# Two cross-attention layers on one core: layer-0 probabilities of 21 subtiles turned by VectorE by way of DRAM, half of their heads' softmax on ScalarE head by head, and the query products ordered a chunk ahead

## The chip, the cores and the metric

The kernel runs on 1 core of one Trainium2 chip. The metric is the device time of one execution in microseconds; the median of several runs is compared. One execution is recorded by the hardware profiler, and its time stands beside its span below.

## The reference

Two cross-attention layers follow each other. `x` is 4 batches of 1024 tokens of width 1024, the context is 4 batches of 64 keys of width 1024, and everything is float32.

```python
# layer 0: 32 query heads of 32, 8 key heads (each serves 4 query heads), 64 keys
q = x @ Wq + bq;  k = ctx @ Wk + bk;  v = ctx @ Wv + bv
scores = einsum("bkgld,bksd->bkgls", q, k) / sqrt(32) + mask
out = einsum("bkgls,bksd->bkgld", softmax(scores), v) @ Wo + bo
x = layernorm(out + x) * gamma + beta
# layer 1: 16 heads of 64; the context is normalized first
a = layernorm(ctx) * g1 + b1
scores = where(mask1, (x @ Wq1.T) (a @ Wk1.T)^T / 8, -inf)
y = x + tanh(gate) * (softmax(scores) (a @ Wv1.T)) @ Wo1.T
```

## The kernel before

**Tiles.** The 4096 tokens are 32 subtiles of 128 (`NSUB`), in 4 blocks of 8 (`SUB`, `NBLK`). Large products are made by Strassen's scheme in Winograd's form: 7 products of half size instead of 8, each of them 4 matmuls of 512 columns accumulated in a PSUM bank. The trace shows twice as many records for a float32 matmul, so one such product is "x8".

**Query products** (`query_steps`, matmul at L536). For a block of 1024 tokens there are 4 chunks `i` of 7 products p1, p2, p6, p7, p5, p3, p4, so 28 steps. They use banks of a PSUM pool `wx` of four. `keep` (L544) is ACT's copy out of a bank with the bias, `add` (L550) is VectorE's addition of a bank to what was kept, and `put` (L547) is the DMA to `qTd` in DRAM, on SP's queue. The rows of the next block are turned by VectorE's 32x32 stream transposes and summed in `rows0`, whose three parts hang on steps 22, 25 and 26.

**Attention of a subtile** (`attend0`). Its queries come from `qTd` (L593), its mask from DRAM (L595). Half `c` of its 32 heads: 16 score matmuls (L604, twice that in records) into the only pair of banks `big`, then VectorE scales them and adds the mask (L609) into a score tile of 1024 per partition, takes the maximum of each head (L453), subtracts it (L461), ACT takes the exponential of the whole tile (L462), VectorE sums (L471), takes the reciprocal (L472) and multiplies (L476).

**Its outputs** (`outputs0`). `flip(c)` turns the probabilities by 8 TensorE transposes per half (L633) into two banks of `one`, which ACT copies out (L634). `values(c)` multiplies them with the values (L639), ACT copies the result (L643), and a DMA takes it to `oTd` (L645).

**Order.** `mix(t, others)` writes the scores of subtile `t`, the outputs of subtile `t - 1` and 3 or 4 query steps of the next block in turn. In the last block (subtiles 24 to 31) the steps are those of `folded_queries` (L737), products of layer-1 weights that no query step needs. The framework's scheduler then settles the order on each engine from this program order; each engine runs its own list in order, and waits on semaphores. A tile waits for whoever used its buffer before. So DMAs issued on one queue, and instructions behind a waiting one on an engine, are held with it.

**After that** come the layer-0 output projection (`project`, L400) with LayerNorm, and layer 1, both full of L400 products. In layer 1 the probabilities of 14 pairs of subtiles are already turned in another way: they are written to DRAM as rows (`p<-s`), read back in quarters of 32 partitions (`load_quarters`, `pq<-p`), both on ACT's queue, and turned within 32x32 blocks by VectorE (`turn_quarters`, L376).

Of the kernel before, what the change touches and what calls it, by code (L numbers as in the profile page):

```python
# [14 lines left out]
P = 128  # L15
# [17 lines left out]
PPB = NPAIR // B  # L33

# [32 lines left out]
def tile_two_cross_attentions(  # L67
# [48 lines left out]
    x1 = [dram.tile([2 * P, H], F32, tag=f"x1_{t}", name=f"x1_{t}") for t in range(NPAIR)]  # L116
    p1 = [dram.tile([2 * P, H], F32, tag=f"p1_{t}", name=f"p1_{t}") for t in range(NPAIR)]
# [191 lines left out]
    for c in range(2):  # L309
# [5 lines left out]
        for j in range(4):  # L315
# [3 lines left out]
                bk_sb[q, c : c + 1], None, ALU.add,  # L319
# [176 lines left out]
    def rows0(blk):  # L496
# [31 lines left out]
        return r, {22: first_half, 25: b12, 26: b22}  # L528

    def query_steps(blk, rows):  # L530

        tmp = {}
# [8 lines left out]
        def keep(name, bank, i, h):  # L541
            t = tmp[name] = etmp.tile([P, HT], F32, tag=name, name=f"{name}_{blk}_{i}")
            m = h * HK + i
            nc.scalar.activation(t, bank, AF.Identity, bias=bq_sb[:, m : m + 1])  # L544

        def put(name, i, h, u):
            nc.sync.dma_start(out=qTd[blk][:, h * HK + i, u * HT : (u + 1) * HT], in_=tmp[name])  # L547

        def add(name, bank, i, h, u):
            nc.vector.tensor_tensor(tmp[name], bank, tmp[name], ALU.add)  # L550
            put(name, i, h, u)

        def p1(i):
            X = tmp["X"] = wx()
# [8 lines left out]
        def p6(i):  # L563
            product(tmp["X"], "S2", "T2", i, False, False)
            keep("z", tmp["X"], i, 1)

        def p7(i):
            V = tmp["V"] = wx()
            product(V, "S3", "T3", i, True, False)

        def p5(i):
            product(tmp["X"], "S1", "T1", i, False, False)
            keep("u", tmp["X"], i, 1)
            add("u", tmp["V"], i, 1, 1)

        def p4(i):
            product(tmp["V"], "A22", "N4", i, False, True)
            add("z", tmp["V"], i, 1, 0)

        def p3(i):  # L580
            product(tmp["X"], "S4", "B22", i, False, True)
            keep("f", tmp["X"], i, 0)
            put("f", i, 0, 1)

        return [lambda i=i, p=p: p(i) for i in range(HK) for p in (p1, p2, p6, p7, p5, p3, p4)]

    probs = {}

    def attend0(t):

        b = t * P // L
        q = qpool.tile([P, KC, P], F32, tag="q", name=f"q0_{t}")
        nc.sync.dma_start(out=q, in_=qTd[t // SUB][:, :, sub_ap(t % SUB)])  # L593
        m = small.tile([P, S], F32, tag="m0", name=f"m0_{t}")
        nc.sync.dma_start(out=m, in_=mask0[sub_ap(t), :])  # L595

        def front(c):
# [10 lines left out]
            s = probs[t, c] = spool.tile([P, 16, S], F32, tag="s", name=f"s0_{t}_{c}")  # L608
            nc.vector.scalar_tensor_tensor(  # L609
# [454 lines left out]
```

## Time and profile before

| | |
|---|---|
| time, median of 3 runs | 1970.59 us (1969.47 to 1971.03) |
| the profiled execution | 1970.75 us, span 1969.0 us, granted TensorE clock 0.993 |
| layer-0 attention, blocks 0 to 2 of subtiles | about 195 to 639 us of the span |
| layer-0 attention, last block | about 639 to 755 us |
| VectorE busy in these two | 353.7 and 102.3 us |
| TensorE transposes of layer-0 probabilities (L633) | 512, 71.4 us busy |
| exponentials of whole score tiles (L462), both layers | 96, mean 1060 ns |

A row of a group gives line, engine and operation, the tiles (out<-in), partitions x elements, the count, then busy time and mean duration of one, then the idle time of the engine just before them and who ended it. Durations of neighbours overlap a little, so a cost per instruction is better read from start to start. PE is TensorE, DVE is VectorE, ACT is ScalarE, POOL is GpSimd and SP is SyncE, which here only issues DMAs.

### The profile page before, as it was taken

What the parts mean: (1) busy time and instruction counts of PE and PEld (TensorE: products, weight loads), DVE (VectorE), ACT (ScalarE), POOL (GpSimd) and SP (SyncE); (2) the same over time, 40 slices, a digit from 0 to 9 for tenths busy, and PEclk for the clock granted to TensorE, in tenths of its full rate; (3) what the DMA queues carried; (4) which work ended last, traced back from release to release, by engine and by line L of the source; (5) the groups of instructions that cost most, each with busy time, mean ns of one, the idle gap of its engine ahead of it and who ended that gap; (6) DMA issues with size and microseconds to landing.
All of it is one profiled execution on the core that took longest, in us unless ns stands there. A gap on an engine that the chain in (4) does not pass through costs nothing.

```text
span 1969.0 us, 16487 instructions
## 1 busy us (share of the span) xinstructions
PE 1929.0 (98%) x6208; PEld 922.9 (47%) x6208; DVE 1273.0 (65%) x1540; ACT 348.6 (18%) x564; POOL 237.6 (12%) x103
## 2 busy tenths in 40 slices
PE   8999999999999999999999999999999999999999
PEld 7744554444454664444443444444444444444443
DVE  3504968598877993455467667657675766576653
ACT  1011333243333672212200000000000000000000
POOL 0000000000000102445455643000000000000000
PEclk9999999999999899999999999999999999999999
DMA  8972226234425888376483335455746574747421
GB/s 276 181 178 71 90 82 161 72 110 120 128 89 192 278 268 288 136 238 226 157 247 119 118 109 126 139 145 154 181 118 161 138 181 118 179 120 181 118 86 43
DMA packets 204559, 301.17 MB, mean 153 GB/s; under 512 B 19136, under 2 KB 134208, under 8 KB 201920
## 3 DMA queue, kind: packets, MB, share of 16 engines
q1 hardware_dynamic: 185216, 270.75, 48.1%
q10 hardware_dynamic: 19264, 29.37, 5.4%
q8 instruction: 49, 0.80, 0.2%
q14 instruction: 30, 0.25, 0.0%
HBM read 182.37 MB, written 117.70 MB: 152 GB/s over the span
## 4 chain that ended last, share of the span: by engine, by line
PE 89%; DVE 8%; DMA 1%; issue 1%; ACT 1%; SPq 0%; DVEq 0%; ACTq 0%
PE wx L400 58%; PE wx L536 17%; PE big L604 2%; PE one L639 2%; PE one L633 2%; DVE s L609 1%; PE wx L350 1%; PE one L350 1%; DVE mx L453 1%; DVE s L461 1%; PE one L764 1%; DVE sm L471 1%; DVE s L476 1%; PE wx L737 1%; PE big L764 1%
## 5 line engine op out<-in xcount | busy, mean ns | idle before, releaser
L408 DVE TENSOR_TENSOR r<-wx,r 128x512 f32<-128x512 f32 x224 | 153.9, 687 | 269.3 <-PE wx L400 262.7
L462 ACT ACTIVATE s<-s 128x1024 f32<-128x1024 f32 x96 | 101.7, 1060 | 748.0 <-DVE s L461 739.3
L789 POOL TENSOR_TENSOR r<-r,bo 128x1024 f32<-128x1024 f32 x32 | 79.1, 2476 | 820.6 <-DMA r<-in_x_dram 819.5
L412 DVE TENSOR_TENSOR s<-wx,key_bias 128x512 f32<-128x512 f32 x64 | 44.2, 690 | 136.9 <-PE wx L400 136.9
L471 DVE TENSOR_REDUCE sm<-s 128x16 f32<-128x1024 f32 x96 | 115.2, 1211 | 22.0 <-ACT s L462 21.5
L536 PE MATMUL wx<-xT,wq_S 128*128 128x512 f32 x256 | 118.9, 605 | 3.1 <-DVE xT L171 3.1
L400 PE MATMUL wx<-wo_B,S 128*128 128x512 f32 x256 | 117.0, 599 | 0.7 <-DVE r L408 0.7
L536 PE MATMUL wx<-xB,wq_A 128*128 128x512 f32 x256 | 117.4, 599 | 0.0
L461 DVE TENSOR_TENSOR s<-s,mx 128x1024 f32<-128x1024 f32 x96 | 116.4, 1213 | 1.1
L453 DVE TENSOR_REDUCE mx<-s 128x16 f32<-128x1024 f32 x96 | 115.5, 1204 | 1.0
L400 PE MATMUL wx<-b_B,pT 128*128 128x512 f32 x256 | 116.1, 593 | 0.0
L400 PE MATMUL wx<-b_B,S_p 128*128 128x512 f32 x256 | 116.0, 596 | 0.0
L400 PE MATMUL wx<-a_B,xT 128*128 128x512 f32 x256 | 115.4, 592 | 0.0
L400 PE MATMUL wx<-a_B,S_x 128*128 128x512 f32 x256 | 115.3, 593 | 0.0
L476 DVE TENSOR_TENSOR s<-s,sm 128x1024 f32<-128x1024 f32 x92 | 113.3, 1240 | 0.9
L400 PE MATMUL wx<-wo_B,o 128*128 128x512 f32 x256 | 113.8, 595 | 0.0
L609 DVE SCALAR_TENSOR_TENSOR s<-big,m 128x1024 f32<-128x1024 f32 x64 | 77.9, 1217 | 31.6 <-PE big L604 31.5
L830 POOL TENSOR_TENSOR r<-r,gamma 128x1024 f32<-128x1024 f32 x32 | 76.1, 2377 | 140.9 <-DVE r L280 140.9
L604 PEld LDWEIGHTS big<-kv,q 64*128 64x128 f32 x1024 | 67.0, 191 | 45.2 <-issue 23.0
L604 PE MATMUL big<-kv,q 64*128 64x128 f32 x1024 | 80.3, 290 | 5.7 <-DMA q<-qTd 2.9
L831 POOL TENSOR_TENSOR r<-r,beta 128x1024 f32<-128x1024 f32 x32 | 80.9, 2528 | 2.4
L634 ACT COPY pT<-one 128x512 f32<-128x512 f32 x128 | 69.3, 595 | 55.9 <-PE one L633 55.7
(152 smaller groups left out, 2689.3 us busy)
## 6 DMA issues: line engine op xcount, KB each, us to landing
xq<-in_x_dram SPq DMA_DIRECT2D x64, 256.0 KB, 9.1
q<-qTd SPq DMA_DIRECT2D x32, 512.0 KB, 4.2
oTd<-oT SPq DMA_DIRECT2D x32, 512.0 KB, 3.6
o<-oTd SPq DMA_DIRECT2D x16, 1024.0 KB, 8.6
ad<-a SPq DMA_DIRECT2D x16, 1024.0 KB, 6.4
r<-in_x_dram SPq DMA_DIRECT2D x32, 512.0 KB, 4.3
bd<-b SPq DMA_DIRECT2D x32, 512.0 KB, 6.6
x<-r SPq DMA_DIRECT2D x32, 512.0 KB, 2.9
```

The costliest lines, as they stand in the source:

```text
L400: nc.tensor.matmul(bank, a[s][:, k, :], w[m][:, k, :], start=first and k == 0, stop=last and k == HK - 1, skip_group_check=True,)
L408: nc.vector.tensor_tensor(at, bank, at, ALU.add)
L453: r = nc.vector.tensor_reduce(mx, s, AX.X, ALU.max)
L461: nc.vector.tensor_tensor(s, s, mx.unsqueeze(2).to_broadcast([P, 16, S]), ALU.subtract)
L462: nc.scalar.activation(s, s, AF.Exp)
L471: nc.vector.tensor_reduce(sm, s, AX.X, ALU.add)
L476: nc.vector.tensor_tensor(s, s, sm.unsqueeze(2).to_broadcast([P, 16, S]), ALU.mult)
L536: nc.tensor.matmul(bank, w_q[a][:, k, sub_ap(i)], rows[b][:, k, :], start=first and k == 0, stop=last and k == HK - 1, skip_group_check=True,)
L604: nc.tensor.matmul(ps[:, at : at + P], q[on, c * 4 + g, :], k0bd[on, b, c, :], start=True, stop=True,)
L609: nc.vector.scalar_tensor_tensor(s, ps.rearrange("p (h s) -> p h s", h=16), SCALE0, m.unsqueeze(1).to_broadcast([P, 16, S]), ALU.mult, ALU ...
L789: nc.gpsimd.tensor_tensor(ru, ru, bo_sb, ALU.add)
L831: nc.gpsimd.tensor_tensor(r[u], r[u], beta0_sb, ALU.add)
```

## The change

1. Subtiles 0 to 20 (`by_turning`) are no longer transposed by TensorE. Their probabilities are written to a DRAM tile `p0` (L773 of the changed kernel), read back by four DMAs into a tile `pq` (L694), all on POOL's queue, and turned by two stream transposes of VectorE (L381). ACT's copies of the transposed banks go with the transposes.
2. A subtile's scores are one tile of 2048 per partition, of which there are two (before: four tiles of 1024). The mask is added by L648. The heads are worked in two groups `e`, the even and the odd ones of each score half. The layout of a turned subtile puts each group's key halves in quarters.
3. In a turned subtile, the 16 heads of group 0 go through ACT one by one (`some`, L662): the negated maximum is the bias, and the accumulator gives the sum. Group 1 keeps the addition (L658), one exponential (L670) and one sum (L675). Maximum (L655), reciprocal (L676) and division (L679) are VectorE's for both groups.
4. The other 11 subtiles keep TensorE's transposes (L704), with the new tiles and groups, and no head by head work.
5. The factor `SCALE0` goes into the keys when they are made. Queries and mask of a subtile are loaded a subtile ahead (`load_queries`, L612 and L615).
6. The query products are ordered with p1 and p2 of chunk `i + 1` ahead of the other five of chunk `i`; what is kept uses three buffers `t` and two `z` (before: two each of four). The first part of `rows0` hangs on step 17.
7. `mix` spreads the steps over five places (six in the first subtile of a block, one of them ahead of the scores) and writes the outputs of `t - 1` later.

```diff
-        return r, {22: first_half, 25: b12, 26: b22}
+        return r, {17: first_half, 25: b12, 26: b22}
...
-        return [lambda i=i, p=p: p(i) for i in range(HK) for p in (p1, p2, p6, p7, p5, p3, p4)]
+        order = [(p1, 0), (p2, 0)]
+        for i in range(HK):
+            order += [(p1, i + 1), (p2, i + 1)] if i + 1 < HK else []
+            order += [(p, i) for p in (p6, p7, p5, p3, p4)]
+        return [lambda p=p, i=i: p(i) for p, i in order]
...
+    def by_turning(t):
+        return t < NSUB - SUB - 3
...
+        s = probs[t] = spool.tile([P, 2048], F32, tag="s", name=f"s0_{t}")
+        if by_turning(t):
+            quarters = s.rearrange("p (a k l) -> p a k l", a=NQ, k=16)
+            heads = s.rearrange("p (e h k l) -> p e k h l", e=2, h=2, k=16)
+        else:
+            quarters = s.rearrange("p (k a l) -> p a k l", a=NQ, k=16)
+            heads = s.rearrange("p (k e h l) -> p e k h l", e=2, h=2, k=16)
+        n = BY_HEAD if by_turning(t) else 0
...
-            nc.vector.scalar_tensor_tensor(
-                s, ps.rearrange("p (h s) -> p h s", h=16), SCALE0,
-                m.unsqueeze(1).to_broadcast([P, 16, S]), ALU.mult, ALU.add,
+            nc.vector.tensor_tensor(
+                quarters[:, :, c * 8 : (c + 1) * 8], ps.rearrange("p (k a l) -> p a k l", a=NQ, l=Q),
+                mask.rearrange("p e (h l) -> p (e h) l", h=2).unsqueeze(2).to_broadcast([P, NQ, 8, Q]),
+                ALU.add,
             )
-            run(softmax_front(s, False, f"0_{t}_{c}"))
+        def largest(e):
+            nc.vector.tensor_reduce(mx[:, e], heads[:, e], AX.XY, ALU.max, negate=True)
+            k = slice(0 if e else n, 16)
+            if k.start < 16:
+                nc.vector.tensor_tensor(heads[:, e, k], heads[:, e, k], wide(mx[:, e, k]), ALU.add)
+        def some(lo, hi):
+            for k in range(lo, hi):
+                nc.scalar.activation(
+                    heads[:, 0, k], heads[:, 0, k], AF.Exp, bias=mx[:, 0, k : k + 1],
+                    accum_out=sm[:, 0, k : k + 1],
+                )
...
+        if by_turning(t):
+            pq = pqpool.tile([P, NQ, 512], F32, tag="pq", name=f"pq0_{t}")
+            v = p0[t].rearrange("(u i) (a w) -> a i u w", i=Q, a=NQ)
+            for a in range(NQ):
+                nc.gpsimd.dma_start(out=pq[a * Q : (a + 1) * Q], in_=v[a])
         def flip(c):
-            pT = pTs[c] = ppool.tile([P, 2, 512], F32, tag="pT", name=f"pT0_{t}_{c}")
+            pT = pTs[c] = ppool.tile([P, 8, P], F32, tag="pT", name=f"pT0_{t}_{c}")
+            if by_turning(t):
+                turn_quarters(pq, pT, (c * 8, (c + 1) * 8))
+                return
...
+        if first:
+            other()
         front(0)
+        if t:
+            flip, values = outputs0(t - 1)
+        if (t + 1) % SUB:
+            load_queries(t + 1)
         other()
         front(1)
+        largest(0)
+        powers(1)
+        largest(1)
+        powers(1)
         other()
         if t:
             flip(0)
+            flip(1)
+        powers(1)
         other()
+        powers(2)
+        total(1)
+        divide(1)
         if t:
             values(0)
+        other()
+        powers(len(exps))
+        total(0)
+        divide(0)
+        if t:
             values(1)
+        other()
+        if by_turning(t):
+            nc.gpsimd.dma_start(out=p0[t], in_=probs[t])
...
-    spool = open_pool(attention, "scores", 4, "right")
-    ppool = open_pool(attention, "probsT", 3, "right")
-    opool = open_pool(attention, "outT", 2, "right")
+    spool = open_pool(attention, "scores", 2, "right")
+    pqpool = open_pool(attention, "probsq", 2, "right")
+    ppool = open_pool(attention, "probsT", 2, "right")
+    opool = open_pool(attention, "outT", 3, "right")
```

## The prediction, made before the changed kernel ran

> **What bounds the kernel now.** I read the page's first part and its chain first, then the groups of instructions, then the windows that cut the layer-0 attention into its blocks.
>
> ```profile
> PE 1929.0 (98%) x6208; PEld 922.9 (47%) x6208; DVE 1273.0 (65%) x1540; ACT 348.6 (18%) x564; POOL 237.6 (12%) x103
> PE 89%; DVE 8%; DMA 1%; issue 1%; ACT 1%; SPq 0%; DVEq 0%; ACTq 0%
> ```
>
> TensorE carries 89% of the chain. Taking work from it pays, if nothing else takes its place. DVE's 8% is what to look for: it lies in the stage that is changed.
>
> ```profile
> core 0: us, PE busy (x) PEld busy (x) DVE busy (x) ACT busy (x) POOL busy (x), PEclk, DMA share, GB/s
> 195.50:342.00 146.50, 144.70 (x666) 73.64 (x666) 118.93 (x119) 53.76 (x81) 0.00 (x0) 1.00 0.41 110
> 342.00:368.00 26.00, 26.00 (x62) 11.10 (x62) 4.94 (x5) 3.21 (x5) 0.00 (x0) 1.00 0.27 86
> 368.00:420.00 52.00, 49.65 (x296) 26.83 (x297) 50.83 (x53) 21.83 (x32) 0.00 (x0) 1.00 0.30 89
> 420.00:499.50 79.50, 78.96 (x346) 38.93 (x346) 69.65 (x68) 29.67 (x46) 0.00 (x0) 1.00 0.48 126
> 499.50:639.00 139.50, 135.51 (x640) 69.77 (x640) 109.31 (x109) 52.53 (x80) 0.00 (x0) 1.00 0.41 131
> 639.00:755.00 116.00, 105.61 (x781) 70.42 (x781) 102.27 (x101) 80.26 (x144) 5.64 (x2) 0.94 0.87 281
> ```
>
> 195.5 to 639 us is subtiles 0 to 23 (443.5 us), mixed with query products; 639 to 755 is the last block, subtiles 24 to 31, mixed with the folded queries. In the first stretch DVE is busy 353.7 us of 443.5, idle 90. It is not idle evenly: between blocks (342 to 368) TensorE runs query products alone and DVE does 5 us in 26; then DVE is the bound (50.8 of 52) while TensorE catches up. POOL does nothing there.
>
> ```profile
> 430.94 3.70 PE L536 MATMUL wx<-xT,wq_S 128*128 128x512 f32 x8
> 434.48 1.04 PE L633 MATMUL one<-ident,s 128*128 128x128 f32 x8
> 435.42 3.70 PE L536 MATMUL wx<-xB,wq_S 128*128 128x512 f32 x8
> 438.95 1.04 PE L633 MATMUL one<-ident,s 128*128 128x128 f32 x8
> 439.83 3.60 PE L536 MATMUL wx<-xN,wq_A 128*128 128x512 f32 x8
> ```
>
> Start to start, a product takes 3.5 us and eight transposes 0.94 and 0.88. The timeline around it gives 1.1 us for the scores of half a subtile and 1.9 for a subtile's values. A block is 28 x 3.5 + 8 x (2.2 + 1.8 + 1.9) = 145 us; measured 443.5 / 3 = 148. So TensorE is full, with some 3 us lost per block.
>
> ```profile
> L471 DVE TENSOR_REDUCE sm<-s 128x16 f32<-128x1024 f32 x96 | 115.2, 1211 | 22.0 <-ACT s L462 21.5
> L462 ACT ACTIVATE s<-s 128x1024 f32<-128x1024 f32 x96 | 101.7, 1060 | 748.0 <-DVE s L461 739.3 <-DVE mx L458 8.4
> L633 PE MATMUL one<-ident,s 128*128 128x128 f32 x512 | 71.4, 283 | 6.8 <-ACT pT L634 4.1 <-DVE s L476 2.7
> L634 ACT COPY pT<-one 128x512 f32<-128x512 f32 x128 | 69.3, 595 | 55.9 <-PE one L633 55.7
> L376 DVE STREAM_TRANSPOSE pT<-pq 128x1024 f32<-128x1024 f32 x28 | 33.1, 1219 | 0.0
> L280 DVE TENSOR_SCALAR r<-r,mv,rstd 128x1024 f32<-128x1024 f32 x32 | 29.3, 917 | 1.1
> ```
>
> **TensorE.** 21 subtiles lose 16 transposes each: 21 x 1.82 = 38 us off the engine that binds. This is the whole of the gain.
>
> **VectorE.** Before, a subtile is 10 instructions over 1024 elements and 2 reciprocals; the dense stretch from 369 to 408 us repeats every 5.8 us per half, so 11.6 per subtile. After, for a turned subtile: 2 adds of the mask, 2 maxima, 1 addition of the negated maximum for the odd heads (for the even ones it is ACT's bias), 1 sum (ACT's accumulator gives the other), 2 reciprocals, 2 divisions, 2 stream transposes. Again 10 and 2: what ACT takes over is what the transposes cost (layer 1's row: 1.22 us each). So DVE stays at about 354 us in the stretch, while TensorE falls to 405: from 80% to 87% of the time. The idle it can afford falls from 90 to 51 us.
>
> What it needs: (a) the block boundary. In the order of instructions the work between the first products after a block's last one and the next block's first scores falls from some 36 us to 25 (34 stationary tiles to 25, 0.88 each, and no transposes), of which DVE's own backlog fills 7 and more; call it 10 idle, three times: 30. (b) Scores write one bank pair, so the second half's scores start only when L648 has emptied the first: 1.1 us plus signalling, 1.25. In about half of the subtiles nothing or one 0.6 us add lies between: some 0.6 us on average, 13 in all. (c) The sum of the odd heads (L675) waits for ACT's 1.06 us exponential with nothing between in some of the subtiles, and the second reciprocal waits for the last of 16 small ones: 0.5 us on average, 11. Together 54 against 51: TensorE and DVE now bind together. I put 5 us on the path for it, with bounds 0 and 30.
>
> **ACT head by head.** No row is of that shape. From rows: 0.20 us fixed (128x1, L276), 0.84 ns per element (L462), 0.09 for a bias that is a pointer (L544 688 ns against L634 595), less 0.12 overlap (two L634 in 1.07): 0.23 us each, 3.7 for 16, against 1.0 for the exponential it replaces. The accumulator may cost another small instruction: 0.1 to 0.2 each, so 3.7 to 7 us per subtile. Four copies (L634, 1.9 us) go. ACT goes from about 6 to 7 or 10 us in 17: not the bound. Its delay is in (c); at 7 us (c) becomes about 1.5 us per subtile, 20 us more.
>
> **The way through DRAM.** 1 MB out and 4 x 256 KB in, on POOL's queue. Nearest rows, on ACT's queue in layer 1:
>
> ```profile
> p<-s ACTq DMA_DIRECT2D x28, 512.0 KB, 2.7
> pq<-p ACTq DMA_DIRECT2D x56, 256.0 KB, 5.2
> ```
>
> A 1 MB write is 4 to 6.4 us (ad<-a is 6.4), the loads 5 to 7, five issues on POOL perhaps 3: 12 to 16 us. In the order of instructions 15 to 30 us of DVE work lie between the division of a subtile and its flips, so they are covered. POOL issues the writes of subtiles 3, 11, 13 and 19 ahead of the loads of the one before; 17 us of DVE work still follow. The other user is the buffer: two score tiles of 2048, so subtile t + 2 may write only when t has left for DRAM. DVE's lead is 5.1 (subtile 10), 6.2 (18) and 6.7 us (2), else 8 to 14, against 5 to 8: some 4 us, partly inside (a). If cover is gone, each us past the lead stands on DVE 21 times. DMA share rises from 0.41 by 2.1 MB per 17 us, 124 GB/s, to below the 0.87 that 639 to 755 shows.
>
> [...]
>
> **A chunk ahead, block by block.** Product order, three `t` and two `z` buffers instead of eight: puts land in 2.0 us and a buffer comes back after about 10, so nothing. The block boundary's shorter run is in (a). The scale moved into the keys, the wider mask (64 KB), the first rows at step 17: 0.
>
> **The subtiles that are not turned.** In the last block DVE binds:
>
> ```profile
> 680.57 1.24 DVE s L609
> ...
> 692.98 1.24 DVE s L609
> ...
> 705.40 1.24 DVE s L609
> ```
>
> The period is 12.41 us with DVE idle under 1. Now the two groups of heads are the even and the odd ones, and both halves of the scores hold some of each, so a maximum needs both halves and in the order nothing separates the two L648: 1.25 us of waiting for scores, 8 times, 10 us. Bounds: 0 (if scores are early) and 18 (if ACT's exponential, now behind two additions, also comes late). I take 10.
>
> **Sum.** Against the profiled execution (span 1969.0, its time 1970.75; the median shown is 1970.59): -38 + 5 + 10 - 1 (fewer switches on TensorE) = -24. 1970.75 - 24 = 1946.75, and about 1946.5 on the median's scale.
>
> **Rivals.** *TensorE's gain handed to DVE.* If (b) and (c) come to 2.5 us per subtile, DVE needs 354 + 30 + 60 = 444 us, as long as the stage now; with the last block's 10 the result is 1955 to 1975, middle 1964. For: DVE already binds from 368 to 412; ACT's keeps stand behind the small exponentials, so a late DVE holds TensorE's banks too. Against: in most subtiles the order puts adds and row transposes into these gaps.
> *The trip through DRAM is late.* If POOL's issue and the transfers take 19 us, 3 us past an average lead of 16 to 18 that remains after queueing, DVE stands at the flips: 21 x 3 = 63 us, less what then is idle anyway (about 15): 1946.5 + 48 = 1995. It decides for slower from about 2 us per subtile. For: no POOL DMA is in this trace, and xq loads of the same size take 9.1 us under load. Against: layer 1 does the same in 8 us on another queue.
> *More gain.* If the boundary idle shrinks to 5 each and last block's waits hide: 1970.6 - 38 - 5 = 1928 or below.
>
> **Numbers.** Main case (1928 to 1957) 0.62; more gain 0.07; handed to DVE 0.19, over half of it still below 1966; late trip 0.12. The range 1924 to 1970 leaves out the late trip and the slow end of the rival. 0.2% is 3.9 us, about what a measurement of this kernel can tell from no change. Faster 0.62 + 0.07 + 0.11 = 0.80, same 0.07, slower 0.13.
>
> **What would show it.** Right: no L633 row for 21 subtiles and the 195 to 640 stretch near 410; DVE over 85% busy in it; a last-block period near 13.7; flips without a DMA as releaser; small exponentials near 0.35 us. Wrong: flips (L381) waiting for pq; L675 or L676 waiting for ACT over 2 us per subtile; a last-block period still 12.4; stretch over 435.

## The result, and the profile after

The changed kernel takes 1966.28 us (median of 20 runs, 1961.63 to 1974.35), the kernel before 1969.53 us beside it (20 runs, 1965.63 to 1972.22): ratio of the means 0.9994, interval 0.9982 to 1.0005. No difference can be measured, where 24 us less were forecast. The profiled execution, 1974.35 us, is the longest of the 20. The runs follow the granted TensorE clock: 1961.63 us had 0.994, 1974.35 us had 0.986.

Parts 1 and 4 of the page (busy time, and the chain of work that ended last) show that the work did leave TensorE; its share of the chain was 89% before.

```profile
PE 1914.1 (97%) x5872; PEld 888.8 (45%) x5872; DVE 1276.1 (65%) x1540; ACT 395.8 (20%) x1131; POOL 295.1 (15%) x208
PE 67%; DVE 6%; DMA 3%; issue 1%; ACT 1%; POOL 0%; SPq 0%; DVEq 0%; ACTq 0%; POOLq 0%
```

6208 - 5872 = 336 matmuls are gone, 21 x 16 transposes. Yet PE's busy time fell by only 15 us, and the span did not fall: TensorE is as busy with less. The windows of the stage show where. The columns are, as before, the stretch and its length, then busy time and count of PE, PEld, DVE, ACT and POOL, then the granted clock, the DMA share and GB/s.

```profile
195.50:342.00 146.50, 140.86 (x534) 62.04 (x534) 117.17 (x118) 69.58 (x295) 22.11 (x40) 1.00 0.85 229
...
368.00:420.00 52.00, 48.67 (x210) 21.98 (x212) 46.74 (x50) 26.58 (x119) 10.97 (x20) 1.00 0.84 226
420.00:499.50 79.50, 74.08 (x282) 32.30 (x282) 62.06 (x58) 33.31 (x137) 10.42 (x19) 0.94 0.80 232
499.50:639.00 139.50, 127.21 (x558) 59.21 (x554) 109.39 (x111) 64.33 (x205) 13.70 (x25) 0.96 0.77 222
639.00:755.00 116.00, 105.42 (x706) 66.51 (x704) 97.08 (x96) 78.58 (x136) 4.99 (x2) 0.90 0.75 240
```

Three columns have changed: the DMA share before 639 us is 0.77 to 0.85 in these rows, where it was 0.30 to 0.48, the clock is below 1.00 in all but two of these stretches, and VectorE is busy 80% of the first stretch and 78% of the one from 499.50, so over the stage it is not the bound either (from 368 to 420 us it comes near, with 90%). From the first score addition of one block to that of the next, the first block of subtiles takes 151.4 us (before 172.4): the gain is there. The second takes 146.2 (before 127.5), the third 142.2 (144.3), and from subtile 24's to subtile 31's it is 102.7 (89.3). What the first block saves, the second and the last give back.

The whole of it, from the first score addition to that of subtile 31, before and after:

```profile
196.68:730.22 533.54, 517.33 (x2641) 277.90 (x2642) 440.50 (x435) 226.03 (x359) 5.64 (x2) 0.99 0.48 144
192.00:734.57 542.57, 505.97 (x2311) 245.74 (x2312) 439.52 (x435) 272.66 (x927) 62.75 (x107) 0.95 0.78 224
```

TensorE idles 36.6 us where it idled 16.2, and the mean clock is lower. By the clock records of the trace it was at half clock for 51 us of this stretch (before 14), so that part of its busy time is the same matmuls at a slower rate: four matmuls of L710 take 1.97 us at 653.96 us (clock 0.50) and 1.08 us at 636.35 us (1.00).

What happens in the second block is seen on SP's queue (timeline of SP: start and duration of the issue in us, line, tiles, count), and then on VectorE and TensorE:

```profile
413.97 6.47 SPq L237 DMA_DIRECT2D xq<-in_x_dram  x3
421.71 2.44 SPq L717 DMA_DIRECT2D oTd<-oT  x2
424.21 3.12 SPq L237 DMA_DIRECT2D xq<-in_x_dram  x3
435.18 1.24 SPq L717 DMA_DIRECT2D oTd<-oT  x2
436.47 1.79 SPq L237 DMA_DIRECT2D xq<-in_x_dram  x2
```

```profile
450.72 1.25 DVE L381 STREAM_TRANSPOSE xT<-xq 128x1024 f32<-128x1024 f32 x1 [5.37 <-DMA xq<-in_x_dram]
```

```profile
455.68 1.23 PE L644 MATMUL big<-kv,q 64*128 64x128 f32 x8 [5.37 <-DVE s L648]
```

Eight row loads belong together. Between the third and the last, SP stands twice at the outputs' puts `oTd<-oT` (L717; a put is the DMA that takes a result to DRAM), which wait for ACT's copy of the values; the longer of these waits, 7.8 us, ends at 435.18. The first row load's own issue also lasts 5.5 us. The last row load starts at 437.22 us, 23 us after the first, and lands after 13.4 us. VectorE waits 5.37 us for these rows, and TensorE then 5.37 us for VectorE. A second stall stands at 575 us, where VectorE waits 4.99 us for a `wo_B` load issued at 567.17 and TensorE 5.01 us for the flip behind it. That load stands less behind a put than behind two DMAs whose issue on SP took 7.09 us (`qTd<-f` at 550.43) and 6.43 us (the mask at 559.48). The waits of SP's queue at the puts between 195 and 640 us, before and after (total, times, longest):

```profile
SPq L645 <- ACT oT L643: 52.7, 18, 6.7
```

```profile
SPq L717 <- ACT oT L716: 148.0, 43, 12.4
```

The change also puts each half of a subtile by itself, 64 puts of 256 KB where there were 32 of 512 KB, so there are more places to wait. And this sum is no measure of the loss: the kernel *turned in place* below has nearly the same one and is 37 us faster than the kernel before.

```profile
SPq L714 <- ACT oT L713: 135.4, 35, 11.9
```

What matters is which load stands behind a wait, and when it is needed.

### The profile page after: what moved, and what is told of

The parts are those of the page before. It is cut to its first block, busy times and chain, and to the rows that moved or that the text cites. A ratio compares the mean times of both kernels' runs of the same rounds, so it can differ in the third digit from the quotient of the medians.

```text
span 1972.6 us, 16687 instructions
## 1 busy us (share of the span) xinstructions
PE 1914.1 (97%) x5872; PEld 888.8 (45%) x5872; DVE 1276.1 (65%) x1540; ACT 395.8 (20%) x1131; POOL 295.1 (15%) x208
## 4 chain that ended last, share of the span: by engine, by line
PE 67%; DVE 6%; DMA 3%; issue 1%; ACT 1%; POOL 0%; SPq 0%; DVEq 0%; ACTq 0%; POOLq 0%
PE wx L405 58%; PE wx L541 3%; PE one L710 2%; PE one L863 1%; DVE sm L675 1%; PE big L644 1%; DVE s L679 1%; DVE mx L655 1%; PE one L704 1%; DVE s L648 1%; PE big L863 1%; PE wx L836 1%; DMA pq<-p 1%; DMA q<-qTd 1%; DMA xq<-in_x_dram 1%
## 5 line engine op out<-in xcount | busy, mean ns | idle before, releaser
L467 ACT ACTIVATE s<-s 128x1024 f32<-128x1024 f32 x32 | 33.7, 1057 | 651.1 <-DVE s L466 642.7
L662 ACT ACTIVATE s<-s,mx 128x64 f32<-128x64 f32 x336 | 111.8, 334 | 60.4 <-DVE mx L655 55.8
L648 DVE TENSOR_TENSOR s<-big,m 128x1024 f32<-128x1024 f32 x64 | 77.5, 1211 | 56.3 <-PE big L644 53.5
L381 DVE STREAM_TRANSPOSE pT<-pq 128x1024 f32<-128x1024 f32 x70 | 82.7, 1217 | 0.0
L710 PE MATMUL one<-pT,kv 128*64 128x512 f32 x256 | 73.0, 667 | 9.0 <-DVE pT L381 8.9
L679 DVE TENSOR_TENSOR s<-s,sm 128x1024 f32<-128x1024 f32 x64 | 78.7, 1248 | 0.5
L405 PEld LDWEIGHTS wx<-wo_B,S 128*128 128x128 f32 x256 | 47.2, 190 | 66.4 <-issue 54.4
```

The source lines that it names most:

```text
L381: nc.vector.transpose(dst.rearrange("p k (u i) -> p k u i", i=Q), t[:, :, k0 * Q : k1 * Q].rearrange("p u (k j) -> p k u j", j=Q),)
L405: nc.tensor.matmul(bank, a[s][:, k, :], w[m][:, k, :], start=first and k == 0, stop=last and k == HK - 1, skip_group_check=True,)
L648: nc.vector.tensor_tensor(quarters[:, :, c * 8 : (c + 1) * 8], ps.rearrange("p (k a l) -> p a k l", a=NQ, l=Q), mask.rearrange("p e (h l) ...
L662: nc.scalar.activation(heads[:, 0, k], heads[:, 0, k], AF.Exp, bias=mx[:, 0, k : k + 1], accum_out=sm[:, 0, k : k + 1],)
L679: nc.vector.tensor_tensor(heads[:, e], heads[:, e], wide(sm[:, e]), ALU.mult)
L710: nc.tensor.matmul(ps[i * 64 : (i + 1) * 64, :], v0bd[:, b, c, i, :], pTs[c][:, i * 4 : (i + 1) * 4].rearrange("p g l -> p (g l)"), start= ...
```

## The experiments

All ratios are to the kernel before, run beside each; 0.1% is 2 us. "The trip" is the way of the probabilities through DRAM, one write and four loads per turned subtile.

**First theory: traffic.** 2.1 MB more per subtile make rows, weights and queries land late. Rivals: the new coupling of VectorE, ACT and TensorE costs the gain, or VectorE binds. Four kernels.

*Turned in place*: the trip is left out, and with it the exchange of 32-row quarters, so the output is not that of the reference.

```diff
-            pq = pqpool.tile([P, NQ, 512], F32, tag="pq", name=f"pq0_{t}")
-            v = p0[t].rearrange("(u i) (a w) -> a i u w", i=Q, a=NQ)
-            for a in range(NQ):
-                nc.gpsimd.dma_start(out=pq[a * Q : (a + 1) * Q], in_=v[a])
+            pq = s.rearrange("p (a w) -> p a w", a=NQ)
...
-        if by_turning(t):
-            nc.gpsimd.dma_start(out=p0[t], in_=probs[t])
```

> Left out of the computation: the exchange of 32-row quarters through DRAM; VectorE turns the probabilities where they lie, so the 1 MB write and the four 256 KB loads of each of the 21 subtiles are gone, everything else of the changed kernel stays. Ratio to the kernel before. Theory 'traffic' (2.1 MB more per subtile make rows, weights and queries land late and hold the score buffers): the loss in 195 to 640 us falls from 56 us to about 30, ratio 0.985 to 0.990. Rival 'coupling' (TensorE waits for VectorE and ACT in the new order, whatever the DMAs do): ratio 0.997 to 1.000, as the changed kernel. Rival 'VectorE bound': the same 0.997 to 1.000, with VectorE over 90% busy.

Measured: 1933.34 us, 0.9814 (0.9801 to 0.9827), 37 us less. Everything except the trip is worth more than the whole forecast, and more than any of the three expectations said. Coupling and a binding VectorE are out as the loss of the changed kernel: the same instructions run on VectorE and ACT here.

*None turned*:

```diff
-        return t < NSUB - SUB - 3
+        return False
```

> No subtile is turned: all 32 go through TensorE's transposes and whole exponentials on ACT, in the changed order (even and odd heads as groups, both additions together, query products a chunk ahead, rows at step 17). Ratio to the kernel before. Theory 'traffic': only the last block costs, about 8 us, so 1.003 to 1.006. Rival 'coupling': the new order alone loses 20 us or more, 1.010 to 1.020. Rival 'order of the query products' (late queries at the block starts): 3 x 3 us and the last block, 1.008, with waits for q at 341, 503 and 630 us.

Measured: 1965.7 us, 0.9978 (0.9970 to 0.9987). Every expectation was wrong in sign: order, grouping and loads a subtile ahead are together a gain of 4 us.

*Whole exponentials*:

```diff
-BY_HEAD = 16
+BY_HEAD = 0
```

> The subtiles are turned through DRAM as in the changed kernel, but the even heads' softmax is whole again (one addition and one sum on VectorE, one exponential on ACT, no accumulator). VectorE gets 2 x 1.2 us more per turned subtile, 50 us in all; ACT loses 16 exponentials of 0.33 and 16 accumulator reads of 0.19 us. Ratio to the kernel before. Theory 'traffic' and rival 'VectorE bound': 1.010 to 1.025. Rival 'coupling by ACT's small exponentials': the waits of the second reciprocal go, 0.995 to 1.003.

Measured: 1963.2 us, 0.9967 (0.9957 to 0.9977). VectorE takes 50 us more work and nothing gets slower: it is far from being the bound in the changed kernel. The figure lies in the range of the rival, small exponentials that hold the second reciprocals; but in the changed kernel these wait 1.0 us for them in all, too little for 5 us. In two faster kernels below the same edit costs 15 and 6 us.

*Traffic beside the kernel before*:

```diff
...
+        if t < NSUB - SUB - 3:
+            nc.gpsimd.dma_start(out=p0[t], in_=kv0)
+            pq = idle.tile([P, NQ, 480], F32, tag="pq", name=f"pq0_{t}")
+            v = p0[t].rearrange("(u i) (a w) -> a i u w", i=Q, a=NQ)
+            for a in range(NQ):
+                nc.gpsimd.dma_start(out=pq[a * Q : (a + 1) * Q], in_=v[a][:, :, 0:480])
...
```

> The kernel before, with traffic that nobody waits for: after each of subtiles 0 to 20 POOL writes 1 MB from a constant tile to DRAM and loads it back in four parts (240 KB each, 480 of 512 columns) to a tile that nobody reads. Theory 'traffic': rows, weights and queries land late as in the changed kernel, plus 8 to 20 us, ratio 1.004 to 1.010. Rivals 'coupling' and 'VectorE bound': within 0.1%, 0.999 to 1.001.

Measured: 2002.18 us, 1.0164 (1.0151 to 1.0177). It looks like a strong yes, and is none. The start of this run (stretch, busy times, clock, DMA share and GB/s):

```profile
0.00:195.00 195.00, 164.58 (x544) 103.92 (x545) 54.35 (x66) 19.56 (x38) 21.75 (x43) 0.93 0.96 296
```

The source tile is a constant, so nothing held these DMAs back: POOL issued all of them by 339 us, and they fell on the loads of the start (share 0.96, clock 0.93), while from 500 to 640 us there was none left (POOL issued nothing, share 0.40). The run answers another question than the one that was asked.

**The theory again, with the pace right.** *Traffic, paced*: the write reads the subtile's own probabilities, so it can't run ahead. Four loads of 240 KB in the next subtile bring them back.

```diff
...
+            for c in range(2):
+                nc.gpsimd.dma_start(
+                    out=p0[t][:, c * 1024 : (c + 1) * 1024], in_=probs[t, c].rearrange("p h s -> p (h s)")
+                )
...
```

> The kernel before, with the trip through DRAM beside its own work, at the changed kernel's pace: after each of subtiles 0 to 20 POOL writes the two halves of its probabilities to DRAM (1 MB), and in the next subtile loads them back in four parts (240 KB each) to a tile that nobody reads; TensorE turns the probabilities as before. Theory 'traffic' (the bytes alone delay rows, weights and queries): slower by 15 to 30 us, ratio 1.008 to 1.016. Rival 'late trip' (what costs is that the flips wait for the exchanged tile): within 0.15%, 0.9985 to 1.0015, since nobody waits for the loads.

Measured: 1971.21 us, 1.0008 (1.0002 to 1.0015): 1.6 us, as the rival "late trip" had it. The DMA share is 0.77 from 195.5 to 342 us and 0.68 from 499.5 to 639 us (changed kernel 0.85 and 0.77), so the pace is nearly the same.

*Trip unread*: the changed kernel with its whole trip, but flips that read the score tile.

```diff
-                turn_quarters(pq, pT, (c * 8, (c + 1) * 8))
+                turn_quarters(s.rearrange("p (a w) -> p a w", a=NQ), pT, (c * 8, (c + 1) * 8))
```

> The changed kernel with its trip through DRAM complete, write and four loads per subtile, but VectorE turns the probabilities where they lie instead of the loaded tile: the exchange of 32-row quarters is left out, and no flip waits for a load. Ratio to the kernel before. Theory 'traffic': as the changed kernel, 0.995 to 1.001. Rival 'late trip': as the kernel that turned in place without a trip, 0.980 to 0.985.

Measured: 1938.84 us, 0.9850 (0.9836 to 0.9864). The first theory falls: with the same bytes under way, 30 of the 37 us are there. Writing and loading unread costs 7 us in this kernel (0.9814 to 0.9850); the other 28 us (0.9850 to 0.9994) come from the flips depending on the trip.

But not as I had put it, by flips that wait for a landing: in the changed kernel no flip waits for `pq` (the last figure is VectorE's idle time before them, 195 to 640 us).

```profile
L381 DVE STREAM_TRANSPOSE pT<-pq 128x1024 f32<-128x1024 f32 x42 | 49.7, 1218 | 0.0
```

The wait has gone into the order instead: the scheduler places the flips well behind the trip. From the end of a subtile's last division to its first flip it is 29.5 us on average in the changed kernel (20 to 40), and 0.9 us with the trip unread. So values, ACT's copies and the puts of the outputs come about one and a half subtiles later, and the puts stand in SP's queue ahead of loads.

*Direct exchange*: 16 DMAs from SBUF to SBUF on POOL's queue, half the bytes, no DRAM.

```diff
...
-            nc.gpsimd.dma_start(out=p0[t], in_=probs[t])
+            pq = turned[t] = pqpool.tile([P, NQ, 512], F32, tag="pq", name=f"pq0_{t}")
+            for a in range(NQ):
+                for u in range(NQ):
+                    nc.gpsimd.dma_start(
+                        out=pq[a * Q : (a + 1) * Q, u], in_=probs[t][u * Q : (u + 1) * Q, a * 512 : (a + 1) * 512]
+                    )
```

> The changed kernel with the exchange made directly from SBUF to SBUF: 16 DMAs of 64 KB per subtile on POOL's queue, right after the division, instead of 1 MB to DRAM and 1 MB back; the output is that of the reference. Half the bytes, and one landing instead of two. Theory 'traffic': half of the 36 us comes back or more, ratio 0.984 to 0.992. Rival 'late trip': one landing of about 5 us plus 16 issues of 0.55 us, nearly as long as the trip, 0.990 to 0.998. [...]

Measured: 1956.08 us, 0.9936 (0.9924 to 0.9948). A third of the 37 us is back, in the range of the rival "late trip". From division to flip it is 14.4 us here, and now VectorE does wait (waits of VectorE, 195 to 640 us):

```profile
DVE pT L381 <- DMA pq<-s: 15.1, 9, 5.7
```

16 issues take POOL 8 us per subtile, and the planned order has some flips ahead of the landing. Whether the earlier order or the smaller traffic makes it faster than the changed kernel, this run does not tell.

*Direct, whole exponentials*: the same with `BY_HEAD = 0`.

> The direct exchange from SBUF to SBUF, and the even heads' softmax whole (one exponential on ACT, VectorE adds and sums all heads). With the trip through DRAM the whole form was 3 us faster than head by head. Theory 'ACT's small exponentials hold the reciprocals and the banks': again 2 to 6 us faster than head by head with the direct exchange. Rival 'VectorE bound': with the exchange out of the way VectorE's 50 us more come onto the path, 5 to 25 us slower than head by head with the direct exchange.

Measured: 1972.49 us, 1.0010 (1.0002 to 1.0018), 15 us slower than head by head, which is what the rival "VectorE bound" had said (5 to 25 us). In the changed kernel the same edit was 5 us faster (0.9994 to 0.9967). The sign of ACT's form hangs on what else waits; here VectorE's 50 us more may well be on the path.

**Second theory: SP held.** The late puts hold SP's queue, and rows, queries and weights behind them start late. Rival: the late order itself leaves TensorE short of work.

*Puts on ACT's queue*, one word changed:

```diff
-            nc.sync.dma_start(out=oTd[t // 2][:, c * 4 : (c + 1) * 4, sub_ap(t % 2)], in_=oT)
+            nc.scalar.dma_start(out=oTd[t // 2][:, c * 4 : (c + 1) * 4, sub_ap(t % 2)], in_=oT)
```

> The changed kernel with one DMA moved: the outputs of a half subtile go to DRAM on ACT's queue, right behind ACT's own copy, instead of on SP's queue. Theory 'SP held' (the turned subtiles' values come up to two subtiles late in the planned order, their puts stand in SP's queue waiting for ACT's copy, and the loads of rows, queries and weights behind them start late): SP's waits for that copy, 171 us in this stage, go; no wait for rows (5.4 us at 445 us) nor for weights (5.0 us at 570 us); 12 to 25 us faster than the changed kernel, ratio to the kernel before 0.986 to 0.993. Rival 'late order' (the late flips themselves leave TensorE short of work, whoever issues the puts): as the changed kernel, 0.997 to 1.001.

Measured: 1947.94 us, 0.9894 (0.9879 to 0.9909): 20 us of the 28. The flips are as late as before, 27.5 us after the division. SP's timeline now has the same eight row loads in a row, with no put between them, merged into one line that begins at 406 us (the last starts 13.6 us behind the first, before 23):

```profile
406.19 13.87 SPq L237 DMA_DIRECT2D xq<-in_x_dram  x8
```

VectorE's waits for `xq` and for `wo_B` are gone from its list.

*Direct exchange, puts on ACT's queue*: both edits.

> The direct exchange from SBUF to SBUF (16 DMAs of 64 KB on POOL's queue) together with the outputs' puts on ACT's queue; the output is that of the reference. Theory 'SP held': the direct exchange alone was 0.9936; 5 to 15 us more come back, 0.985 to 0.991. Rival 'late order': 0.993 to 0.995, as the direct exchange alone.

Measured: 1966.48 us, 0.9989 (0.9979 to 0.9999), a clear miss: 10 us slower than the direct exchange with the puts on SP's queue. TensorE waits 17.5 us for flips here, in 11 places. Its flips are 13.6 us behind the division, so "late values" alone don't make the moved puts a gain. Why this order is so much worse I can't say.

*Late in place*: no trip, but flips and values one subtile later in the program (flips of `t - 2` instead of `t - 1`), three score buffers.

> No trip through DRAM: VectorE turns the probabilities where they lie (the exchange of 32-row quarters is left out), but flips and values of a turned subtile are written one subtile later in the program, with three score buffers; in the planned order a flip then stands about half a subtile to one later than in the in-place kernel, still earlier than in the changed kernel. Theory 'SP held' and rival 'late order' both put it between the in-place kernel (0.981) and the changed one: 0.984 to 0.992. If it stays at 0.980 to 0.983, lateness up to one subtile is free, and the loss belongs to the two-subtile lateness or to the transfers.

Measured: 1936.77 us, 0.9835 (0.9822 to 0.9848), between the two ranges that were expected (0.984 to 0.992 for a loss, 0.980 to 0.983 for none). Flips stand 8.7 us behind the division, and that costs 4 us against the in-place kernel, with intervals that overlap.

*By half*: the 11 subtiles that are not turned, again with 16 heads of one score half as a group.

```diff
-            heads = s.rearrange("p (k e h l) -> p e k h l", e=2, h=2, k=16)
+            heads = s.rearrange("p (e k h l) -> p e k h l", e=2, h=2, k=16)
...
+        if not by_turning(t):
+            largest(0)
+            powers(1)
         other()
         front(1)
-        largest(0)
-        powers(1)
+        if by_turning(t):
+            largest(0)
+            powers(1)
         largest(1)
```

> The changed kernel, with the 11 subtiles that are not turned worked again by halves of the scores (16 heads of one half as a group, its maximum, addition and exponential written ahead of the second half's scores) instead of even and odd heads. Theory of the last block: the second addition of the mask no longer waits 1.26 us for scores, the period of the last block falls from 13.2 to 12.4 us, 5 to 8 us faster than the changed kernel, ratio to the kernel before 0.994 to 0.998. Rival: the wait is filled otherwise, no difference, 0.998 to 1.001.

Measured: 1965.16 us, 0.9984 (0.9976 to 0.9991), not distinguishable from the changed kernel, as the rival had it. In the last block the changed kernel showed the wait that was forecast (timeline of VectorE):

```profile
723.89 1.22 DVE L648 TENSOR_TENSOR s<-big,m 128x1024 f32<-128x1024 f32 x1 [1.26 <-PE big L644]
```

With the halves this wait is gone (the first half now waits 1.1 us), and the period is 13.6 us instead of 13.2: TensorE and ACT then take turns (transposes wait for ACT's copies, up to 1.4 us, and the next scores stand behind them).

**Is the held queue a matter of this change?** *The kernel before, puts on ACT's queue*: the same word changed there.

> The kernel before, with its outputs' puts on ACT's queue instead of SP's. Theory 'SP held by the change' (the puts hold SP only because the turned subtiles' values are late): within 0.3% of the kernel before, 0.997 to 1.002. Rival 'SP is held in any case' (the move is a gain of its own, of the same size before and after): 0.985 to 0.992, and then it says nothing of where the change's gain went.

Measured: 1968.28 us, 0.9993 (0.9985 to 1.0002). Nothing, as the theory has it.

*In place, puts on ACT's queue*:

> No trip through DRAM (VectorE turns the probabilities where they lie; the exchange of 32-row quarters is left out), and the outputs' puts on ACT's queue. Theory 'SP held by late values': here values are early, so the move of the puts is worth under 4 us, ratio to the kernel before 0.979 to 0.983. Rival 'SP is held in any case': 10 us or more faster than in place with the puts on SP's queue, under 0.977.

Measured: 1937.78 us, 0.9836 (0.9818 to 0.9855). Nothing again, or a loss of up to 4 us (the range expected ended at 0.983). Where values are early, as in these two kernels, puts on SP's queue did no harm.

*Puts on ACT's queue, whole exponentials*:

> The changed kernel with the outputs' puts on ACT's queue, and the even heads' softmax whole (one exponential, VectorE adds and sums all heads). On SP's queue the whole form was 3 us faster than head by head. Theory 'ACT's small exponentials hold ACT's copies, and with them the puts': the gain goes with the puts' move, so this is 3 to 15 us slower than head by head with the puts on ACT's queue, ratio to the kernel before 0.991 to 0.997. Rival 'small exponentials hold VectorE's reciprocals and TensorE's banks whatever the puts do': 2 to 6 us faster, 0.986 to 0.989.

Measured: 1955.71 us, 0.9927 (0.9910 to 0.9944), 6 us slower than head by head, in the theory's range. But that VectorE's 50 us more are on the path here, as in the direct exchange, would give the same sign, so this run does not tell the two apart.

*Puts on ACT's queue, the write held behind the loads*:

```diff
-            nc.gpsimd.dma_start(out=p0[t], in_=probs[t])
+            tc.keep_in_program_order(nc.gpsimd.dma_start(out=p0[t], in_=probs[t]))
```

> The changed kernel with the outputs' puts on ACT's queue, and the write of a subtile's probabilities on POOL's queue held behind the loads of the subtile before (in the planned order of the changed kernel some writes stand ahead of these loads and hold them for up to 8 us). Theory 'late trip' for the 9 us that still lie between the kernel with the puts on ACT's queue and the one whose trip nobody waits for: 3 to 8 us faster than without this, ratio to the kernel before 0.985 to 0.988. Rival: the loads are early enough anyway, 0.988 to 0.991.

Measured: 1964.11 us, 0.9974 (0.9959 to 0.9989), 16 us slower, where 3 to 8 us less were expected. The edit touches one DMA on POOL, but VectorE's order changed with it: flips stand 31.4 us behind the division (27.5 without the hold). This is a warning for every comparison here: a DMA that is moved or held can also change the order of TensorE's and VectorE's instructions.

*Loads on ACT's queue*, the counter-test: puts stay, rows of blocks 2 and 3 and all queries leave SP's queue.

```diff
-            load_quarters(xq, x[at : at + 2 * P, :])
+            load_quarters(xq, x[at : at + 2 * P, :], nc.scalar if blk > 1 else nc.sync)
...
-        nc.sync.dma_start(out=q, in_=qTd[t // SUB][:, :, sub_ap(t % SUB)])
+        nc.scalar.dma_start(out=q, in_=qTd[t // SUB][:, :, sub_ap(t % SUB)])
```

> The changed kernel with its outputs' puts left on SP's queue, but the loads that stand behind them moved away: the rows of blocks 2 and 3 and the queries of every subtile are loaded on ACT's queue. Theory 'SP held' (the puts do no harm by themselves, the loads behind them do): most of what the moved puts gave, 10 to 22 us faster than the changed kernel, ratio to the kernel before 0.988 to 0.995; ACT may stall for landed queries at three block starts, up to 4 us each. Rival 'the planned order' (moving a DMA makes the scheduler settle TensorE's and VectorE's order anew, and that alone made the difference): no side is preferred, 0.995 to 1.006.

Measured: 1976.92 us, 1.0036 (1.0025 to 1.0047). The theory's figure (0.988 to 0.995) is missed; that of the rival, a new planned order (0.995 to 1.006), is met. The waits of ACT (195 to 757 us) say in part why:

```profile
ACT oT L716 <- DMA xq<-in_x_dram: 19.3, 2, 9.6
```

SP is still held at the outputs' puts (123.5 us from 195 to 640 us, 148.0 in the changed kernel), now with query puts and the `wo_B` loads behind it (VectorE waits 8.8 us for `wo_B`, TensorE 10.7 us for queries), and ACT's copies stand twice behind row loads. So this run moved the hold and did not remove it. It speaks for the rival, but does not refute the theory.

**The best version.** *Puts on ACT's queue and halves*:

> The two edits that helped, together: the outputs' puts on ACT's queue, and the 11 subtiles that are not turned worked by halves of the scores. Alone they gave ratios of 0.9894 and 0.9984 to the kernel before. If the gains of the two add, 0.986 to 0.989; if the order of the last block, bound by TensorE's and ACT's turn-taking with a period of 13.2 to 13.6 us, is what limits both, 0.988 to 0.991.

Measured: 1939.37 us, 0.9846 (0.9831 to 0.9862), 30 us faster than the kernel before. It beats both. Against the puts alone the halves give 9 us here (0.9894 to 0.9846), most of it from subtile 24 to 27 (41.0 us against 46.1, with TensorE at half clock for 7 us against 17); the period at the end stays 13.2 us.

## Why the prediction was wrong, point by point

**TensorE's 38 us: right in kind, too large in size.** 336 records are gone. Counted at full rate, TensorE's work in the stage fell by 26 to 29 us (table below). That the kernel turned in place is 37 us faster matches 38 by luck: less idle time and less half clock than before are part of it. The 1 us more for fewer switches on TensorE was an estimate, and no run shows it.

**VectorE and TensorE bind together, +5: too pessimistic.** VectorE's work is the forecast 354 us, but that is 80% of a stage that did not get shorter, not over 85%. Its waits for scores are 42.7 us from 195 to 640 us: 18.3 at the three block starts, where (a) put 30, and 24.4 inside the blocks, where (b) put 13. For (c) it is 17.4 us at ACT's exponential (L675) and 1.0 at the second reciprocal, where 11 were put. Turned in place the waits for scores are 23.1 us, the second block takes 125.1 us against 127.5 before, and TensorE idles less than before (table below). There the waits fit into idle time. That VectorE took 50 us more (whole exponentials) without loss holds for the changed kernel alone: in two faster ones the same edit cost 15 and 6 us, so the margin is not large.

**ACT head by head: the size was right.** A small exponential lasts 334 ns, and the accumulator is read by an instruction of its own, 187 ns, that overlaps; start to start 0.333 us, 5.3 us for 16, inside the 3.7 to 7 put down.

```profile
L662 ACT ACTIVATE s<-s,mx 128x64 f32<-128x64 f32 x336 | 111.8, 334 | 60.4 <-DVE mx L655 55.8
```

**The last block, +10: near in sum by luck, wrong in its cause.** Subtile 24 to 31 cost 13.4 us more. The period rose from 12.41 to 13.2, not 13.7: about 4 us, which is also what the whole stretch costs with the trip unread (93.5 us against 89.3). The rest is between subtiles 24 and 27 (49.4 us, before 39.7; 40.5 with the trip unread and 41.9 with the halves). The granted clock in this stretch is 0.73 where it was 0.85 before and 0.98 with the trip unread; 0.27 of 49.4 us against 0.15 of 39.7 is some 7 us, an estimate, so most of the rest is lost clock. Why the clock fell there more is open. And the wait of 1.26 us, there as forecast, was not the price: taken away, it left the period where it was or longer.

**The way through DRAM, "covered": this step failed.** Everything but the trip gives 37 us; the trip takes 35 of them (0.9814 to 0.9994), and the sum had put it at nothing. Its parts were near: 5.9 us for the write, 7.1 us for the loads, four issues 2.2 us.

```profile
p<-s POOLq DMA_DIRECT2D x21, 1024.0 KB, 5.9
pq<-p POOLq DMA_DIRECT2D x84, 256.0 KB, 7.1
```

That no flip would wait for a DMA was right too. What I asked was only whether VectorE has enough to do between division and flip. I did not ask what stands behind the flips: values, ACT's copy, and a put on the queue on which the rows of the next block, the queries and the weights are loaded. The cover made the flips wait for nobody, and in the planned order that meant the flips 29.5 us behind the division, and this put later still. On SP's queue the put that waited 7.8 us until 435.18 us had the last two row loads behind it; they were issued from 436.47 us on. The rival "the trip is late" named the right part with the wrong place: nothing stood at the flips.

**The DMA share "below 0.87": right as a figure (0.77 to 0.85), and nearly harmless**: 1.6 us beside the kernel before, 7 us in the changed one.

**VectorE's transposes weighed against TensorE's.** Two stream transposes take 2.25 to 2.28 us from start to start (at 263.44 and 244.33 us), where 16 transposes of TensorE took 1.82. In engine time the change so loses some 9 us in 21 subtiles, an estimate; turned in place it gains 37, because TensorE binds and VectorE has room. But that leaves out the exchange of quarters, which only VectorE's way needs; POOL's issue takes 550 ns in all 84 loads of it (longest 572). With it nothing is left: with none turned the kernel is at 0.9978, with 21 subtiles turned at 0.9994. The kernel as changed would have done no worse with TensorE's transposes in every subtile.

**Where the gain went.** The stage from the first score addition to that of subtile 31 can be split for each profiled execution, by the clock records and TensorE's busy time: what the busy time would be at full rate, what was lost of it at half clock, and idle time (us).

| kernel | stage | at full rate | lost at half clock | idle |
|---|---|---|---|---|
| before | 533.5 | 510.6 | 6.7 | 16.2 |
| changed | 542.6 | 481.9 | 24.1 | 36.6 |
| changed, puts on ACT's queue | 514.0 | 484.4 | 9.2 | 20.3 |
| trip unread | 509.3 | 483.5 | 4.5 | 21.3 |
| turned in place | 499.5 | 483.6 | 3.4 | 12.5 |

So TensorE's work did fall, by 26 to 29 us in all four. In the changed kernel 20 us more of idle time and 17 us more at half clock took it back, and moving the puts returned 16 and 15 of them. The changed kernel's profiled execution is its slowest, so its half-clock loss is on the high side.

**How sure is the cause?** Shown: most of the loss is neither the traffic nor the engines' own work, but comes with the flips depending on the trip (trip unread), and moving the outputs' puts brings back 20 of these 28 us in this kernel, and nothing in either kernel with early values. The trace shows the stalls that go: 5.4 us for rows, 5.0 us for `wo_B`.

Not shown: that the 20 us are these stalls and what follows them, and that the puts' waits made them. SP's own issues from 195 to 640 us take 130 us in the changed kernel, 78 with the puts moved, 91 turned in place; long issues held the `wo_B` load more than a put did. With the trip unread VectorE waits even 8.8 us for `wo_B`, and no single wait of TensorE in that stretch is longer than 4.6 us. A new order comes with a moved or held DMA, and the held write shows 16 us that may be nothing else. Moving the puts cost 10 us in the direct exchange, and the counter-test with the loads moved came out as the rival said. No run has flips 29 us late without a trip. The last 9 us between the moved puts and the unread trip stay open.

## What to carry to other kernels

When a transfer is hidden behind other work, follow its consumers to the end: where the scheduler puts them, which DMAs they issue, and what is queued behind those DMAs. Try stores that wait for an engine's copy on that engine's own queue rather than in front of loads on a shared one; one word changed tests it. Here it gave 20 us in the changed kernel, nothing in two kernels with early values, and a loss of 10 us in the direct exchange, so it has to be measured each time. And give test traffic a real dependency, or it runs where nobody asked for it (in the first traffic test POOL issued all of it by 339 us).

## What the runs showed of the hardware

**An idle TensorE was paid twice.** After the 5.37 us at 450 us the granted clock (third column from the end) is low for 10 us:

```profile
450.00:455.00 5.00, 0.32 (x1) 0.00 (x0) 4.28 (x6) 0.00 (x0) 0.00 (x0) 0.83 0.41 140
455.00:460.00 5.00, 4.32 (x16) 2.02 (x18) 5.00 (x5) 0.58 (x1) 0.56 (x1) 0.50 0.53 213
460.00:465.00 5.00, 5.00 (x15) 2.17 (x12) 3.05 (x4) 0.58 (x1) 2.18 (x4) 0.65 0.82 194
465.00:470.00 5.00, 5.00 (x13) 2.13 (x13) 5.00 (x6) 4.55 (x24) 0.00 (x0) 1.00 1.08 301
```

At 0.50 and 0.65 some 4 us of work are lost in these 10 us, on top of the wait (half of 4.32 us and 0.35 of 5.00, an estimate). The clock also fell after shorter gaps. Behind one of 1.84 us (and one of 1.16 us five us earlier) it is at half for the next 13.7 us, though TensorE is busy for 13.64 of them:

```profile
647.86 1.97 PE L704 MATMUL one<-ident,s 128*128 128x128 f32 x8 [1.84 <-DVE s L679]
```

```profile
647.80:661.50 13.70, 13.64 (x46) 7.46 (x48) 10.22 (x9) 7.08 (x11) 2.65 (x1) 0.50 0.61 208
```

Half of 13.64 us is some 6.8 us of lost work, an estimate. So in this trace a gap of 1.84 us was paid twice, like the one of 5.37 us. I had counted every stall once. The busy time of the half-clocked TensorE also hid the loss: PE's share stayed at 97%. With the puts moved, 420 to 500 us runs at 1.00 (420 to 499.5 in the changed kernel at 0.94).

**Issuing a DMA took up to 7.09 us by itself.** The mask load on SP in the changed kernel, 195 to 640 us (min, median and max of its issue, in ns):

```profile
L615 SPq DMA_DIRECT2D m<-in_mask_dram x24: 372/595/6429, 196.3 to 612.6; - x24
```

Another issue, `qTd<-f` at 550.43 us, lasts 7.09 us. In the kernel before the mask's longest is 657 ns. The mask is twice as wide after, but turned in place the same load's longest issue in this stretch is 1132 ns, and with the trip unread it is 3605 ns. With the paced traffic beside the kernel before the narrow one's is 657. So issues of 3 us and more were seen in this stretch only where the changed kernel's own DMAs and the trip through DRAM came together; the cause stays open. They held SP in addition to its waits: its issues in this stretch take 130 us in the changed kernel.
